# Silu slices of a background generator get a slot of their own, and the order of a selective scan's side work is rearranged

## The chip, the cores and the metric

The kernel runs on one core of a Trainium2 chip. The metric is device time in microseconds (us) of one execution, the median of several runs. Five engines of the core matter here: TensorE (PE in the profile), VectorE (DVE), ScalarE (ACT), GpSimd (POOL) and SyncE (SP), whose queue issues the DMAs. Each engine works through its own instructions in the order in which the program lists them, and waits on semaphores for the others.

## The reference

Sixteen images of 64 x 64 x 96 go through two residual blocks, all in float32.

```python
x = x + _L0_conv_ref(_gn(x), L0_conv_W1, L0_conv_b1, L0_conv_W2, L0_conv_b2, L0_conv_coef)
x = x + _L1_conv_ref(_gn(x), L1_conv_in_proj_w, L1_conv_conv_w, L1_conv_conv_b, ...)
```

The first block upsamples twofold by Fourier transform, applies a two-layer perceptron with a quadratic activation, filters and downsamples. The second block is a state-space layer: an input projection, a 3 x 3 depthwise convolution with Silu, four scan directions over the 4,096 positions, a layer norm, a Silu gate and an output projection. Its core is

```python
delta = jax.nn.softplus(dts + dt_bias[None, :, :, None])
...
def step(h, inps):
    dt, ut, bt, ct = inps
    h = jnp.exp(dt[..., None] * As[None]) * h + (dt * ut)[..., None] * bt[:, :, None, :]
    y = jnp.einsum('bkdn,bkn->bkd', h, ct)
    return (h, y)
```

for 192 channels, 16 states and 4 directions.

## The kernel before, in words

**The scan loop.** `scan` (from line 615) cuts the work into units. A unit holds 32 channels x 4 states as 128 partitions, in two halves `e` of the channels, over `T` = 1,024 positions. Four units (`j`) make a block of all 16 states, six blocks a step, eight steps an image: 192 units an image, 3,072 in all. Directions are taken in pairs: the backward pair scans the same tiles from the end.

Per unit the engines do this:

- ScalarE, `decay` (L755): `da` = exp(delta x A), 128 x 1024, into one of two buffers in PSUM (pool `sc_aps`, `bufs=2`).
- GpSimd, `drive` (L761): `b` = dtu x B for both halves at once, 128 x 2048, two units ahead; `b` has four buffers.
- VectorE, `recur` (L770 forward, L772 backward): the recurrence, by a scan instruction. Half 1 writes its result over `b`, half 0 over `da`.
- The product of the state with C: half 0 on VectorE (L924), half 1 on GpSimd (L915). Every fifth unit (`SHARE = 5`, `odd_here`), half 1 scans into `da` as well and its product is done on VectorE too (L906), so that GpSimd has one product less.
- ScalarE or VectorE, `keep` (L778): a copy of the last column, the state for the next step.
- TensorE, `read_out` (L794): sums over states, a unit later, 16 small matmuls into `y`; after a block, ScalarE copies `y` out (`store`, L805).

In the program, a unit `n` runs: scan of half 1, `decay(n+1, 1)`, position 0; product of half 1 on GpSimd, `drive(n+2)`, scan of half 0, `read_out(n-1)`, position 1; product of half 0, `keep`, `decay(n+1, 0)`, perhaps the copy of `y`, position 2.

**The side work.** Everything else is written as Python generators, whose pieces are put between the scan's instructions at the three positions of each unit, by `Background.slot`. A generator counts the weight of its pieces (1, or `HEAVY` = 2) and is given its next piece whenever it is behind an even spread: `SLICES` = 550 weights over the 576 positions of an image for `front` and `finish`, `PSLICES` = 71 over the 72 positions of a step for `project`. A piece that yields `WAIT` is followed by one that may stand at position 2 only.

- `front(mi)` does the first block of the next image and the start of the second. It works in strips of `PP` = 25 upsampled rows: `fetch_x` loads pieces `xr` of the image (L303), TensorE widens them (L324), groups of `PG` = 5 rows go through the perceptron (L365, L348, L377), then the rest. Its last part is the convolution with nine taps (L482), then a matmul for the gate (L494), then one slice with `Silu` for both (L500, L501). Silu is in another table of ScalarE than exp and log, so a table load stands on each side of it: one at L500, one by `preload_act_table_set(BOTH)` at L502. There are 12 such slices per image: 8 for the channels 0 to 127 (`i` = 0), 4 for the other 64 (`i` = 1, two halves of the image beside each other). The results go to DRAM, and `turn` (L467) makes a transposed copy `col`.
- `project(mi, pair, lc, out)` makes `delta` and `dtu` = delta x u for the next step: a projection `pp` (L655), copied to `pr` (L659), then for three channel groups a matmul (L666), a softplus in six ScalarE instructions (L674 to L681), a sum of four terms by identity matmuls on TensorE (L686), `dtu` on VectorE (L691), `delta` copied by ScalarE (L692), both stored to DRAM and later loaded spread over partitions (`spread`, L703).
- `finish(mi)` does the layer norm, gate and output projection of the image before.

The first `project` runs to its end before the scan begins, and so does the first `front`; the last `finish` runs after it. Loads and stores are all issued from SyncE's queue, in program order. Tiles named `piece` (11 buffers) are shared by all the side work; `b16` and `b18` have one buffer each and hold the image-sized tiles.

Of the kernel before, what the change touches and what calls it, by code (L numbers as in the profile page):

```python
# [54 lines left out]
UPS = 100  # L55
# [16 lines left out]
SLICES = 550  # L72
WAIT = -1
HEAVY = 2
# [5 lines left out]
def tile_two_blocks(  # L80
# [159 lines left out]
    def front(mi):  # L240
# [71 lines left out]
        o_last = None  # L312
        for p0 in range(0, UPS, PP):

            t1 = b18.tile([HW, PP, C], F32, name="t1", tag="b18")
            xr = fetch_x(0)
            for _ in range(3):
                yield
            for cg in range(3):
                u_ps = [bank([HW, 16, PP], "u_ps") for _ in range(2)]  # L320
                for k in range(16):
                    for a in range(2):
                        on = slice(64 * a, 64 * a + 64)
                        nc.tensor.matmul(  # L324
                            u_ps[a][:, k, :], lhsT=xr[k // 8][on, k % 8, :], rhs=up_s[on, p0:p0 + PP],
                            start=True, stop=True,
                        )
                    if k == 7:
                        yield
                if cg < 2:  # L330
                    xr = fetch_x(cg + 1)
                yield
                for a in range(2):
                    c0 = 48 * a + 16 * cg
                    nc.scalar.copy(t1[:, :, c0:c0 + 16], u_ps[a].rearrange("w c p -> w p c"))
                    yield
# [4 lines left out]
            for g in range(PP // PG):  # L341
# [8 lines left out]
                for j in range(HB + 1):  # L350
                    if j == 0 and o_last is not None:
                        keep_o(o_last)
                    elif j == 1 and len(t2) == 2:
                        square(0)
                        d_ps = narrow()
                        yield
                        sd = piece([128, PG * C], "sd")
                        nc.scalar.copy(sd, d_ps)
                    elif j:
                        square(j - 1)  # L360
                    if j == 2 and sd is not None:
                        stow(sd, row - 2 * PG)
                    if j < HB:
                        h_ps[j] = bank([128, PG * UPS], "h_ps")
                        nc.tensor.matmul(  # L365
                            h_ps[j], lhsT=w1t_s[:, 128 * j:128 * (j + 1)],
                            rhs=xu.rearrange("c p q -> c (p q)"), start=True, stop=True,
                        )
                    elif g < PP // PG - 1:
                        xu_ps = widen(t1, g + 1)  # L370
                    yield
# [89 lines left out]
        for i, n, tiles, both in ((0, 128, 8, 0), (1, 64, 4, 4)):  # L461
# [14 lines left out]
            for t in range(tiles):  # L476
                c_ps = bank([128, 8, HW], "c_ps")
                for tap in range(9):
# [8 lines left out]
                    if tap == 2 and turned is not None:  # L487
                        turn(*turned)
                    if tap % 3 == 2 and tap < 8:
                        yield HEAVY  # L490
# [13 lines left out]
                yield HEAVY  # L504
# [14 lines left out]
    def finish(mi):  # L519
# [19 lines left out]
        for t in range(8):  # L539
# [7 lines left out]
            for ob, n in ((0, 128), (1, 64)):  # L547
                oc = slice(128 * ob, 128 * ob + n)
                y_ps = bank([n, 8, HW], "yc")
                for i, (w, of) in enumerate(((pmat_s[:, 0, oc], y0), (pd_s[:, 0, oc], u0), (pd_s[:, 1, oc], yu))):  # L550
                    nc.tensor.matmul(  # L551
                        y_ps, lhsT=w, rhs=of.rearrange("c (h w) -> c h w", w=HW), start=(i == 0), stop=False
                    )
                if tail is not None:
                    tail = next(tail, None) and tail
# [3 lines left out]
                yield HEAVY  # L559
# [18 lines left out]
            yield HEAVY  # L578
# [5 lines left out]
            yield HEAVY  # L584
# [30 lines left out]
    def scan():  # L615


        with ExitStack() as es:
# [9 lines left out]
            banks.append(es.enter_context(tc.tile_pool(name="b_ps", bufs=2, space=PSUM)))  # L628
            aps = es.enter_context(tc.tile_pool(name="sc_aps", bufs=2, space=PSUM))
            yps = es.enter_context(tc.tile_pool(name="sc_yps", bufs=1, space=PSUM))  # L630
            gps = es.enter_context(tc.tile_pool(name="sc_gps", bufs=1, space=PSUM))

            def project(mi, pair, lc, out):
# [3 lines left out]
                out["rows"] = rows = dctx.tile([2, 2 * NS, T], F32, name="rows")  # L637
                out["delta"] = [dctx.tile([128, T], F32, name=f"delta_d{v}") for v in range(3)]
                out["dtu"] = [dctx.tile([128, T], F32, name=f"dtu_d{v}") for v in range(3)]
                xs_d = image[mi]["xs"]  # L640
                order = (0, 2, 1)

                def fetch_u(v, t):
                    uv = up_.tile([128, TB], F32, name="u")
                    nc.sync.dma_start(out=uv, in_=xs_d[v, :, lc * T + t:lc * T + t + TB])
                    return uv

                ahead_u = [fetch_u(v, 0) for v in order]
                for _ in range(4):
                    yield  # L650
                for t in range(0, T, TB):
                    u, ahead_u = dict(zip(order, ahead_u)), []
                    pp = gps.tile([128, TB], F32, name="pp", tag="g")
                    for v in range(3):
                        nc.tensor.matmul(pp, lhsT=xpt_s[:, pair, v, :], rhs=u[v], start=(v == 0), stop=(v == 2))  # L655
                    for _ in range(2):
                        yield
                    pr = pj.tile([128, TB], F32, name="pr")
# [3 lines left out]
                    for i, v in enumerate(order):  # L662
                        if i == 0:
                            yield
                        s = gps.tile([128, TB], F32, name="s", tag="g")
# [6 lines left out]
                        yield  # L672
                        e, d, m, w = (pj.tile([128, TB], F32, name=k) for k in ("e", "d", "m", "w"))
                        nc.scalar.activation(e, s, AF.Abs)  # L674
                        nc.scalar.activation(e, e, AF.Exp, scale=-1.0)
                        yield
                        nc.scalar.activation(m, s, AF.Relu)
                        nc.scalar.activation(w, e, AF.Identity, bias=one_s)
                        yield
# [3 lines left out]
                        s = gps.tile([128, TB], F32, name="s", tag="g")  # L683
# [3 lines left out]
                        for _ in range(3):  # L687
                            yield
                        dtu = pj.tile([128, TB], F32, name="dtu")
                        delta = pj.tile([128, TB], F32, name="delta")  # L690
# [6 lines left out]
                        if t + TB < T and i < 2:  # L697
# [40 lines left out]
            for _ in project(*steps[0], ctxs[0]):  # L738
                pass
            bc = {(what, 0, j): fetch_bc(ctxs[0], 0, j, what) for j in range(NQ) for what in range(2)}  # L740
            dtus = {0: fetch_dtu(ctxs[0], 0)}
            deltas = {(0, e): fetch_delta(ctxs[0], 0, e) for e in (1, 0)}
# [79 lines left out]
            class Background:  # L822

                def __init__(self, gen, slices, positions):
                    self.gen, self.slices, self.positions, self.at, self.n = gen, slices, positions, 0, 0
                    self.wait = False

                def slot(self, position):  # L830
                    self.at += 1
                    if self.wait and position < 2:
                        return
                    if self.gen is not None and self.n * self.positions < self.at * self.slices:
                        self.step()

                def step(self):
                    weight = next(self.gen, 0)
                    if weight == 0:
                        self.gen = None  # L840
                    else:
                        self.wait = weight == WAIT
                        self.n += 1 if weight in (None, WAIT) else weight

# [5 lines left out]
            ahead_gen = behind_gen = step_gen = nothing  # L850

            def slot(position):
                step_gen.slot(position)
                (ahead_gen if ahead_gen.gen is not None else behind_gen).slot(position)

            last = len(units) - 1
            def next_step(st, mi):

                nonlocal step_gen
                if st < len(steps):  # L860
                    if steps[st][0] > mi:
                        ahead_gen.drain()
                    step_gen = Background(project(*steps[st], ctxs[st]), PSLICES, 3 * per_step)
# [6 lines left out]
            storing = None  # L870

            for n, (st, bi, j) in enumerate(units):
# [29 lines left out]
                odd_here = n % SHARE == SHARE - 1  # L902
# [157 lines left out]
```

## Time and profile before

| | |
|---|---|
| time, median of 3 runs (lowest, highest) | 21502.07 us (21501.11, 21510.08) |
| profiled execution | 21508.85 us, span 21507.1 us |
| scan, first to last scan instruction | 536.2 to 21342.0 us |
| `da` decay, ScalarE L755 | 6144 of 1116 ns |
| scans, VectorE L770 and L772 | 6144 of 2280 to 2347 ns |
| products, VectorE L924 / L906 | 3072 of 1223 ns / 614 of about 1224 ns |
| `drive`, GpSimd L761 | 3072 of 4536 ns |
| product of half 1, GpSimd L915 | 2458 of 2361 ns |
| table loads in the scan, ScalarE L500 and L502 | 180 + 180 of 1283 ns |
| DMA | 4277 MB, mean 199 GB/s |

In the profile's lines, `DVE b L770 <- ACT da L755` reads: VectorE's instruction at line 770 that writes `b` waited for ScalarE's at line 755 that writes `da`. A group of instructions has its count after an `x`. Scans that write `b` are those of half 1, scans that write `da` those of half 0 (and of half 1 in every fifth unit). A window gives for each engine its busy us and, in brackets, its instructions. A timeline row has start, duration and engine; durations of two neighbours on VectorE and on ScalarE overlap by about 0.1 us.

### The profile page before, as it was taken

The numbers are of one execution on the slowest core, as the hardware profiler recorded it, in microseconds if no ns is written. First come the engines' busy times: TensorE is split into PE (matmuls) and PEld (weight loads), VectorE is DVE, ScalarE is ACT, GpSimd is POOL, SyncE is SP. The second block draws the span as 40 slices with busy tenths as digits, with TensorE's granted clock in tenths as the row PEclk, the third lists the DMA queues.
The fourth block names the chain that finished last, engine by engine and source line by source line (L and its number), as shares of the span: only waits on it lengthen the run. The fifth ranks groups of instructions, "written<-read, shape, count | busy, mean of one in ns | idle before, by whom it ended". The sixth has DMA issues, their size and how long they took to land. (4 is left out here: it accounts for less than half of the span.)

```text
span 21507.1 us, 273615 instructions
## 1 busy us (share of the span) xinstructions
PE 16918.9 (79%) x98988; PEld 7271.3 (34%) x98988; DVE 19512.2 (91%) x12983; ACT 13741.5 (64%) x20546; POOL 19511.8 (91%) x5538
## 2 busy tenths in 40 slices
PE   7776877878878788787878778788787888878855
PEld 4423324233332333324333242333423333243221
DVE  0999999999999999999999999999999999999997
ACT  3666666667666666666666666676666666666553
POOL 0999999999999999999999999999999999999996
PEclk8887888888889888898888888888898888888877
DMA  2565565656656566565655656566565665656654
GB/s 74 180 207 184 199 224 187 217 192 204 217 189 227 187 218 203 187 228 183 219 197 200 224 191 215 192 208 215 185 227 187 211 203 192 230 184 217 222 186 140
DMA packets 1855466, 4277.13 MB, mean 199 GB/s; under 512 B 449438, under 2 KB 548670, under 8 KB 1852062
## 3 DMA queue, kind: packets, MB, share of 16 engines
q1 hardware_dynamic: 1854110, 4259.62, 58.8%
q8 instruction: 781, 12.80, 0.2%
q14 instruction: 575, 4.71, 0.1%
HBM read 3380.58 MB, written 878.18 MB: 198 GB/s over the span
## 5 line engine op out<-in xcount | busy, mean ns | idle before, releaser
L761 POOL TENSOR_TENSOR b<-dtu,bt 128x2048 f32<-128x2048 f32 x3072 | 13905.1, 4536 | 594.2 <-DMA dtu<-dtu_d 530.5
L755 ACT ACTIVATE da<-delta,a_s 128x1024 f32<-128x1024 f32 x6144 | 6852.3, 1116 | 2859.4 <-DVE b L924 888.2
L915 POOL TENSOR_TENSOR b<-b,ct 128x1024 f32<-128x1024 f32 x2458 | 5804.1, 2361 | 1235.6 <-DVE new L778 832.6
L794 PE MATMUL y<-b,fold_s 128*32 128x256 f32 x49152 | 3837.1, 435 | 1111.6 <-DVE b L924 551.4
L924 DVE TENSOR_TENSOR b<-da,ct 128x1024 f32<-128x1024 f32 x3072 | 3756.5, 1223 | 93.9
L770 DVE TENSOR_TENSOR_SCAN da<-da,new,b 128x1024 f32<-128x1024 f32 x1383 | 3246.5, 2347 | 282.8 <-ACT da L755 274.7
L772 DVE TENSOR_TENSOR_SCAN da<-da,new,b 128x1024 f32<-128x1024 f32 x1382 | 3242.4, 2346 | 125.5 <-ACT da L755 119.1
L794 PEld LDWEIGHTS y<-b,fold_s 128*32 128x32 f32 x49152 | 1392.0, 119 | 3857.0 <-issue 1333.0
L778 ACT COPY new<-da 128x1 f32<-128x1 f32 x2764 | 434.6, 157 | 2786.4 <-DVE b L924 2294.7
L772 DVE TENSOR_TENSOR_SCAN b<-da,new,b 128x1024 f32<-128x1024 f32 x922 | 2157.9, 2341 | 47.0 <-ACT da L755 46.1
L770 DVE TENSOR_TENSOR_SCAN b<-da,new,b 128x1024 f32<-128x1024 f32 x921 | 2156.6, 2342 | 41.1 <-ACT da L755 39.5
L482 PE MATMUL c_ps<-xgp,wtap_s 96*128 96x512 f32 (+1 forms) x4608 | 1721.3, 642 | 203.6 <-ACT row L500 199.1
L686 PE MATMUL s<-w,ident_s 128*128 128x512 f32 x1536 | 1175.4, 857 | 872.0 <-ACT w L681 752.3
L666 PE MATMUL s<-pr,dtw_s 128*128 128x512 f32 x1536 | 939.0, 696 | 544.6 <-ACT delta L692 328.0
L365 PE MATMUL h_ps<-xu,w1t_s 96*128 96x500 f32 x1920 | 1059.4, 652 | 306.7 <-ACT hsq L348 124.2
L377 PE MATMUL o_ps<-w2c_s,hsq 128*100 128x96 f32 x9600 | 1031.9, 266 | 170.0 <-ACT hsq L348 143.7
L772 DVE TENSOR_TENSOR_SCAN da<-da,b 128x1024 f32<-128x1024 f32 x461 | 1055.9, 2291 | 118.4 <-ACT da L755 116.7
L770 DVE TENSOR_TENSOR_SCAN da<-da,b 128x1024 f32<-128x1024 f32 x460 | 1053.4, 2290 | 106.5 <-ACT da L755 104.3
L377 PEld LDWEIGHTS o_ps<-w2c_s,hsq 128*100 128x100 f32 x9600 | 966.1, 178 | 357.2 <-ACT hsq L348 184.9
L686 PE MATMUL s<-e,ident_s 128*128 128x512 f32 x1536 | 1022.9, 755 | 0.0
L482 PEld LDWEIGHTS c_ps<-xgp,wtap_s 96*128 96x128 f32 (+1 forms) x4608 | 600.1, 172 | 1154.9 <-issue 873.0
L787 PE MATMUL y<-y,ident_s 128*128 128x512 f32 x768 | 534.1, 784 | 538.6 <-ACT yt L805 537.1
(128 smaller groups left out, 21920.7 us busy)
## 6 DMA issues: line engine op xcount, KB each, us to landing
dtu<-dtu_d SPq DMA_DIRECT2D x1536, 512.0 KB
delta<-delta_d SPq DMA_DIRECT2D x1536, 512.0 KB
bt<-rows SPq DMA_DIRECT2D x1024, 512.0 KB
ct<-rows SPq DMA_DIRECT2D x1024, 512.0 KB
u<-xs_d SPq DMA_DIRECT2D x896, 256.0 KB
dtu_d<-dtu SPq DMA_DIRECT2D x768, 256.0 KB
delta_d<-delta SPq DMA_DIRECT2D x768, 256.0 KB
xr<-in_x SPq DMA_DIRECT2D x768, 128.0 KB
```

The source lines that it names most:

```text
L365: nc.tensor.matmul(h_ps[j], lhsT=w1t_s[:, 128 * j:128 * (j + 1)], rhs=xu.rearrange("c p q -> c (p q)"), start=True, stop=True,)
L377: nc.tensor.matmul(o_ps[:, p, :], lhsT=hsq[j][:, UPS * p:UPS * (p + 1)], rhs=w2c_s[:, j, :], start=(j == 0), stop=(j == HB - 1),)
L482: nc.tensor.matmul(c_ps[p:p + n], lhsT=wtap_s[:, tap, 128 * i:128 * i + n], rhs=xgp[:, h0:h0 + 8, dx:dx + HW], start=(tap == 0), stop=(tap ...
L666: nc.tensor.matmul(s, lhsT=dtw_s[:, pair, v, :], rhs=pr, start=True, stop=True)
L686: nc.tensor.matmul(s, lhsT=ident_s, rhs=of, start=(k == 0), stop=(k == 3))
L755: nc.scalar.activation(da, deltas[n // NQ, e], AF.Exp, scale=a_s[:, k, g, units[n][2]:units[n][2] + 1])
L761: nc.gpsimd.tensor_mul(b, dtus[n // NQ], bt.unsqueeze(1).to_broadcast([128, 2, T]))
L770: nc.vector.tensor_tensor_scan(out, da, b, before, ALU.mult, ALU.add)
L772: nc.vector.tensor_tensor_scan(out[:, ::-1], da[:, ::-1], b[:, ::-1], before, ALU.mult, ALU.add)
L794: nc.tensor.matmul(y[32 * q:32 * q + 32, e, :], lhsT=fold_s, rhs=b[:, e, QT * q:QT * q + QT], start=(pair == 0 and j == 0 and e == 0), sto ...
L915: nc.gpsimd.tensor_mul(h, h, bc[1, r, j])
L924: nc.vector.tensor_mul(bs[n][:, 0, :], h, bc[1, r, j])
```

## The change

- `Background` no longer skips positions itself. One function `slot` decides for both generators. A Silu slice (after `WAIT`) may come only at position 2, with no copy of `y` pending in the unit; then `full` keeps `project`'s pieces that follow a `BUSY` mark out of this position and the next, and `full_unit` makes the next unit one with both products on VectorE. A `project` that is behind may have two pieces at one position, if neither follows a `BUSY`.
- Units with both products come by `credit`: one is taken at every fifth unit as before, and one forced by a slice is paid back later.
- In `project`, the pieces with ScalarE work are marked `BUSY`.
- The convolution is cut into pieces of two taps (weight 1) instead of three (weight 2), the 64-channel part comes first, and several `HEAVY` yields of `finish` become plain ones, one of them new. `SLICES` is 499.
- `fetch_x` is called earlier: two fetches are in flight, and those of the next strip start in the last group of the strip before.
- The first `project` becomes two generators, one for each half of the 1,024 positions, that take turns; the second works in tiles of its own (`far_u`, `far_w`), in the two image-sized buffers. PSUM for it comes from a pool of its own with four banks. The first loads for the scan are issued once both halves have made their first channel group.

```diff
-SLICES = 550
+SLICES = 499
 WAIT = -1
+BUSY = -2
...
+        asked = []
         for p0 in range(0, UPS, PP):
...
-            xr = fetch_x(0)
-            for _ in range(3):
-                yield
+            if not asked:
+                asked += [fetch_x(0), fetch_x(1)]
+                for _ in range(3):
+                    yield
             for cg in range(3):
+                xr = asked.pop(0)
...
-                if cg < 2:
-                    xr = fetch_x(cg + 1)
+                if cg == 0:
+                    asked.append(fetch_x(2))
...
+                    if j >= 2 and g == PP // PG - 1 and p0 + PP < UPS:
+                        asked.append(fetch_x(j - 2))
...
-        for i, n, tiles, both in ((0, 128, 8, 0), (1, 64, 4, 4)):
+        for i, n, tiles, both in ((1, 64, 4, 4), (0, 128, 8, 0)):
...
-                    if tap == 2 and turned is not None:
+                    if tap == 3 and turned is not None:
                         turn(*turned)
-                    if tap % 3 == 2 and tap < 8:
-                        yield HEAVY
+                    if tap % 2 == 1:
+                        yield
...
-                        yield
+                        yield BUSY
                         e, d, m, w = (make(k) for k in ("e", "d", "m", "w"))
                         nc.scalar.activation(e, s, AF.Abs)
                         nc.scalar.activation(e, e, AF.Exp, scale=-1.0)
-                        yield
+                        yield BUSY
...
-            for _ in project(*steps[0], ctxs[0]):
-                pass
...
+            far_u = b16.tile([128, 4, TB], F32, name="far_u", tag="b16")
+            far_w = b18.tile([128, 6, TB], F32, name="far_w", tag="b18")
...
+            with tc.tile_pool(name="side_ps", bufs=4, space=PSUM) as side:
+                todo = [project(*steps[0], ctxs[0], side, 0), project(*steps[0], ctxs[0], side, TB, far.get)]
+                while todo:
+                    todo = [g for g in todo if next(g, todo) is not todo]
+                    if ctxs[0]["made"] >= 2 and not dtus:
+                        bc[0, 0, 0] = fetch_bc(ctxs[0], 0, 0, 0)
+                        dtus[0] = fetch_dtu(ctxs[0], 0)
+                        for e in (1, 0):
+                            deltas[0, e] = fetch_delta(ctxs[0], 0, e)
...
             def slot(position):
-                step_gen.slot(position)
-                (ahead_gen if ahead_gen.gen is not None else behind_gen).slot(position)
+                nonlocal full, full_unit
+                back = ahead_gen if ahead_gen.gen is not None else behind_gen
+                back.at += 1
+                step_gen.at += 1
+                gate = back.said == WAIT and back.due() and position == 2 and storing is None
+                if gate:
+                    full, full_unit = 2, n + 1
+                if step_gen.due() and not (full and step_gen.said == BUSY):
+                    light = step_gen.said != BUSY
+                    step_gen.step()
+
+                    if light and step_gen.due() and step_gen.said != BUSY:
+                        step_gen.step()
+                if back.due() and (gate or back.said != WAIT):
+                    back.step()
+                full = max(full - 1, 0)
...
-                odd_here = n % SHARE == SHARE - 1
+
+                credit += 1
+                odd_here = n == full_unit or credit >= SHARE
+                if odd_here:
+                    credit -= SHARE
```

## The prediction, made before the change was run

> **What bounds the kernel now.** I read the page's busy times first, then what VectorE and GpSimd wait for inside the scan (536 to 21342 us), then one image cut into four stages, then timelines.
>
> ```profile
> PE 16918.9 (79%) x98988; PEld 7271.3 (34%) x98988; DVE 19512.2 (91%) x12983; ACT 13741.5 (64%) x20546; POOL 19511.8 (91%) x5538
> ```
>
> The first five lines of VectorE's waits in the scan and the first of GpSimd's (us in total, times, longest):
>
> ```profile
> DVE da L770 <- ACT da L755: 379.0, 366, 3.4
> DVE da L772 <- ACT da L755: 235.8, 240, 4.0
> DVE dtu L691 <- PE s L686: 235.0, 129, 13.3
> DVE b L772 <- ACT da L755: 177.6, 88, 4.7
> DVE b L770 <- ACT da L755: 72.6, 58, 22.0
> ```
>
> ```profile
> POOL b L915 <- DVE new L778: 832.6, 438, 16.0
> ```
>
> VectorE and GpSimd are equally busy, and each idles about 1,300 us of the scan's 20,806. But VectorE hardly waits for GpSimd (23 us in all), while GpSimd waits for VectorE. So VectorE's chain sets the time: its work plus its waits for ScalarE (865 us) and TensorE (235 us). Time saved on GpSimd alone is worth nothing until those waits are gone.
>
> The stages of the image scanned from 4450 us on: its units 0 to 95, 96 to 139 (the Silu slices of the next image), 140 to 167, 168 to 191.
>
> ```profile
> core 0: us, PE busy (x) PEld busy (x) DVE busy (x) ACT busy (x) POOL busy (x), PEclk, DMA share, GB/s
> 4449.80:5101.50 651.70, 502.79 (x3706) 261.05 (x3706) 605.81 (x399) 434.42 (x699) 611.25 (x174) 0.82 0.58 195
> 5101.50:5407.90 306.40, 256.63 (x1192) 95.11 (x1192) 275.30 (x189) 218.61 (x300) 279.01 (x80) 0.89 0.63 206
> 5407.90:5595.30 187.40, 168.70 (x717) 55.42 (x718) 183.06 (x135) 113.16 (x171) 178.05 (x51) 0.93 0.70 233
> 5595.30:5748.80 153.50, 125.41 (x572) 41.04 (x570) 152.30 (x93) 90.25 (x115) 150.22 (x44) 0.89 0.66 216
> ```
>
> VectorE idles 46, 31, 4 and 1 us in them: there is little to gain after unit 140.
>
> A Silu slice that happens to stand before a unit with both products on VectorE, on ScalarE and then on VectorE:
>
> ```profile
> 2714.99 1.12 ACT L755 ACTIVATE da<-delta,a_s 128x1024 f32<-128x1024 f32 x1
> 2716.13 1.28 ACT L500 ACT_TABLE_LOAD   x1
> ...
> 2718.62 1.28 ACT L502 ACT_TABLE_LOAD   x1
> ...
> 2720.10 1.12 ACT L755 ACTIVATE da<-delta,a_s 128x1024 f32<-128x1024 f32 x1
> ```
>
> ```profile
> 2717.14 1.23 DVE L906 TENSOR_TENSOR b<-da,ct 128x1024 f32<-128x1024 f32 x1
> 2718.28 2.35 DVE L772 TENSOR_TENSOR_SCAN da<-da,new,b 128x1024 f32<-128x1024 f32 x1
> 2720.66 1.22 DVE L924 TENSOR_TENSOR b<-da,ct 128x1024 f32<-128x1024 f32 x1
> ```
>
> The next decay ends at 2721.22, the product at 2721.88: VectorE does not wait, with 0.6 us to spare.
>
> **What the Trainium skill says.** "ScalarE: Activation LUTs", What ACT_TABLE_LOAD costs, has about 1,283 ns for a load and some 1,380 ns of drain with it. The trace agrees on the load (1.28 us), but shows no drain beside it: the block of two loads and two activations takes 3.8 us here (2716.13 to 2719.90). "Perfetto Trace Analysis", Tensor Engine Instruction, says ScalarE, VectorE and GpSimd are strict FIFO; the decays behind the Silu block bear it out. "SBUF — State Buffer", two separate sides, says a VectorE instruction with two SBUF inputs and a GpSimd instruction lock each other out. The 96x1 product at line 236 fits: median 4.1 us, longest 12.0. Its count doesn't change; only its alignment to GpSimd will.
>
> **The Silu slices.** There are 180 in the scan. I joined each with VectorE's idle time before the first scan two units later, the first instruction that needs a decay queued behind it: 239 us in all. With nothing else in the slice and TensorE in time, 60 lose 0.08 us each; 15 followed by a unit with both products lose nothing. The loss is in three other groups: softplus pieces in the same slot (81 us), a y copy there (25 us), and 48 that wait for the convolution's last matmuls (ScalarE's row waits 107.8 us for them), which lose 127 us. In the changed program's order every one of the 180 has only the two loads and the two activations between its decays, and the following unit has both products. The first two groups go: -106 us. The TensorE group shrinks. Its last piece before the slice is 2 matmuls, not 4, of 0.97 us (in units 98 to 115 of the image above, 64 full-width matmuls, two records each, occupied TensorE for 61.8 us); so a row that came 3.0 us late comes about 1.1 late, and 0.6 is spare: 0.5 us at perhaps 60 slices, 30 us. Bounds 0 and 130 (no better than now). Together -209.
>
> **Second scans.** Of the 615 us before scans that write `da`, 479 us are 477 units that lose 1.00 us each: there the decay of half 0 was given the PSUM bank of half 1, so it starts only when this unit's first scan ends. Counting banks in the changed program gives 527: +50 us. In units 0 to 95 this is 1.3 us less per image (288 against 309 of them in the run); in 96 to 139 it is 12 per image against 7.2. The change doesn't touch the cause.
>
> **dtu.** 235 us wait for the softplus sums on TensorE, 73 of them in units 108 to 114, where three-tap pieces stand ahead. With two-tap pieces I take 2 us per image for 4.8 in that stage and 1.3 less per image elsewhere; the TensorE work per unit is only slightly more even (392 two-unit stretches above 12 us against 453, by durations of the trace). Bounds: all 235 stays, or 100 is left. The softplus steps themselves move little: 75 are held back, 153 pairs share a slot, nearly all of them DMA issues or a bare allocation.
>
> **The units with both products.** 614 in both kernels: they move. In 96 to 139 they become 13 for 9; the debt leaves 141 to 167 with none. An ordinary unit is 5.89 us of VectorE (starts 2.36, 2.37, 1.14 apart, and a copy in three of four) and 6.80 of GpSimd (4.49 and 2.31); one with both is 6.91 and 4.49.
>
> - Units 96 to 139, VectorE: before 35 x 5.89 + 9 x 6.91 + 44 x 0.15 (dtu) = 275.0, idle 32.5 by the mean over images, 307.5; measured mean 307.8. After: 31 x 5.89 + 13 x 6.91 + 6.6 = 279.0; idle 12 second scans, 2 Silu, 2 dtu, 1.3 others, 3.3 in gaps under 0.1 us: 20.6; in all 299.6. GpSimd needs 269. So -8.2 per image: 12 us of waits less, 4 us of work more.
> - Units 140 to 167: GpSimd becomes the bound, 27 x 6.80 + 4.49 = 188.1 against 189.0 measured (mean). VectorE needs some 183 and runs ahead.
> - Units 168 to 191: the last stage of an image now holds more of `finish` (it ends at unit 190, not 185). VectorE 159 less the 5 it is ahead, against 153.3. Both stages: -0.5.
> - Units 0 to 95: -1.3 and -1.3 as above.
>
> Sum: -11.3 per image, 15 images: -170 us.
>
> **First projection.** Now 430 to 536 us: six softplus rounds of 12 us in series, 515, then DMAs; the first decay waits until 533.97 for its delta. After: the second half's u goes into the buffer of `col`, whose 2 MB must first be stored (10 us at the page's mean of 199 GB/s); that holds both, since the halves alternate on TensorE. Then three double rounds of 19 us (7.8 ScalarE, 11 TensorE) and 8 us for `pp`: 430 + 10 + 8 + 57 = 505, with delta and dtu fetched long before. First scan at 508: -25, bounds -10 and -45. Earlier xr fetches in the first front: TensorE waits 7.1 us for them: -5. Inside the scan they are covered.
>
> Smaller weights and `SLICES` 499 only spread the same work: `front` ends at unit 141 for 135, `finish` still ends inside its image. The tail is the same.
>
> **Sum.** -170 - 30 = -200. From the profiled execution's 21508.9 us: 21309; the median of the runs shown is 6.8 lower: 21302.
>
> **Rivals.**
> 1. TensorE is late for the slices all the same. Pieces now come one a slot, and 105 of 180 slices stand one slot after the last piece (75 before). For: 48 waits now. Against: half-size pieces. If 105 lose 0.9 us and GpSimd's stretch costs 5 us more an image (95 + 75): 21302 + 170 - 30 = 21442, hardly a gain.
> 2. Slower: fetches of xr in the last group of a strip ask for pieces while all 11 are in use, and SyncE's queue, in order, holds delta loads behind them. Now decays wait 60.3 us for delta; SyncE already waits up to 13.0 us for a piece's reader. It decides when each of 3 strips holds delta loads 6 us past their lead: 18 x 15 = 270, so 21572. Against: the count of xr loads that wait for TensorE hardly rises (208 for 197).
> 3. More gain: slices lose nothing, dtu waits drop to 100, the projection gives 45: 21302 - 30 - 75 - 20 = 21177.
> 4. The delays do nothing because softplus isn't due near the slices: excluded, the changed program's order shows the slices bare.
>
> **Chances.** Forecast 0.58 (own range 21220 to 21400), rival 1 0.16, rival 2 0.09, rival 3 0.17. A measurement tells 0.2% (43 us) from no change. Rival 1 splits about evenly across 21459, so faster 0.83, same 0.08, slower 0.09. The range leaves out most of rival 2 and the ends of 1 and 3: 21120 to 21470.
>
> **What would show it.** First-scan waits (`b` L770, L772) fall from 250 to near 50; waits of `da` scans rise a little, from 615 towards 665; GpSimd without a gap in units 141 to 167; the first scan near 508 us. It is wrong if row still waits for c_ps over 100 us with the first scans idle, or if decays wait for delta much above 60 us.

## The result and the profile after

| | before | after |
|---|---|---|
| median (lowest, highest), us | 21503.11 (21501.11, 21510.08) | 21328.53 (21321.19, 21346.15) |
| profiled execution, its span | 21508.85, 21507.1 | 21326.15, 21324.4 |
| start of the scan; its length | 536.2; 20805.8 | 495.9; 20662.7 |

The ratio is 0.992, interval 0.9906 to 0.9934: faster by 175 us, against 200 forecast. Of the 183 us between the two profiled executions, 40 come from the earlier start of the scan and 143 from a shorter scan. The new numbers of the lines spoken of: decay L788, drive L794, scans L803 (forward) and L805 (backward), products L972, L954 and L963, dtu L702, row L506, the norm's product L237.

The page's busy times after, to compare with the first line shown before:

```profile
PE 16949.4 (79%) x98988; PEld 7262.1 (34%) x98988; DVE 19510.9 (91%) x12983; ACT 13759.8 (65%) x20546; POOL 19511.8 (91%) x5538
```

VectorE has as much to do as before, to 1.3 us. The gain is in its waits. Each unit has two scans: the first is that of half 1, the second that of half 0. VectorE's waits after, in the scan (us in total, times, longest):

```profile
DVE da L803 <- ACT da L788: 305.7, 318, 1.9
DVE da L805 <- ACT da L788: 287.4, 251, 4.5
DVE dtu L702 <- PE s L697: 143.6, 95, 13.8
...
DVE b L805 <- ACT da L788: 98.2, 69, 3.8
...
DVE b L803 <- ACT da L788: 20.8, 22, 1.7
```

First scans (`b`) lose 119 us for 250, `dtu` 144 for 235, while the `da` scans still lose 593 us for 615. The four stages of the image scanned from 4400 us on, cut at the same units as before:

```profile
4399.60:5033.10 633.50, 496.10 (x3702) 258.62 (x3702) 602.97 (x393) 424.06 (x660) 607.57 (x173) 0.84 0.57 195
5033.10:5344.30 311.20, 250.52 (x1183) 91.86 (x1184) 286.90 (x195) 226.15 (x338) 272.49 (x77) 0.87 0.59 194
5344.30:5531.90 187.60, 157.13 (x693) 51.63 (x692) 177.35 (x131) 114.29 (x168) 185.14 (x55) 0.92 0.78 259
5531.90:5689.30 157.40, 139.70 (x610) 45.40 (x608) 154.24 (x95) 93.43 (x120) 153.22 (x44) 0.95 0.66 219
```

The stage that was to gain, the second, became longer: 311 us for 306, with VectorE busy 287 for 275. The first became 18 us shorter. Means over 14 images, the second to the fifteenth, say the same (us per image; the last three columns are kernels of the experiments below):

| units | before | after | before, own buffers | after, own buffers | best kernel |
|---|---|---|---|---|---|
| 0 to 95 | 655.3 | 637.7 | 633.9 | 624.9 | 624.8 |
| 96 to 139 | 307.6 | 310.7 | 296.6 | 309.6 | 297.4 |
| 140 to 167 | 189.2 | 188.6 | 185.4 | 189.2 | 185.8 |
| 168 to 191 | 153.3 | 157.5 | 153.3 | 157.0 | 153.0 |

A Silu slice that TensorE did not reach in time, on ScalarE, VectorE and TensorE (`row` is what the slice's first activation writes, `c_ps` the convolution's result that it reads):

```profile
5256.94 1.28 ACT L506 ACT_TABLE_LOAD   x1
5262.42 0.69 ACT L506 ACTIVATE row<-c_ps,convb_s 128x512 f32<-128x512 f32 x1 [4.19 <-PE c_ps L488]
```

```profile
5266.60 2.35 DVE L805 TENSOR_TENSOR_SCAN b<-da,new,b 128x1024 f32<-128x1024 f32 x1 [3.45 <-ACT da L788]
```

```profile
5250.52 4.65 PE L488 MATMUL c_ps<-xgp,wtap_s 96*128 96x512 f32 x8
5255.01 1.02 PE L697 MATMUL s<-w,ident_s 128*128 128x512 f32 x2
...
5257.59 1.02 PE L697 MATMUL s<-m,ident_s 128*128 128x512 f32 x2
5258.44 1.88 PE L488 MATMUL c_ps<-xgp,wtap_s 96*128 96x512 f32 x4
5261.26 1.13 PE L488 MATMUL c_ps<-xgp,wtap_s 96*128 96x512 f32 x2
```

The reader sees an empty ScalarE: after the table load it stands 4.19 us for the last taps, and the decay behind it makes VectorE's next scan 3.45 us late, in spite of the 1.23 us product put in between. On TensorE the four sums of a softplus (5255.0 to 5258.4) lie between two pieces of the convolution: keeping softplus from ScalarE's slot does not keep it from TensorE's queue. There are 60 such late rows in the scan, 124 us in all; before there were 48, with 108 us.

### The profile page after: what moved, and what is told of

Read it like the earlier page. It is cut to its first block, busy times and chain, and to the rows that moved or that the text cites. A ratio compares the mean times of both kernels' runs of the same rounds, so it can differ in the third digit from the quotient of the medians.

```text
span 21324.4 us, 273404 instructions
## 1 busy us (share of the span) xinstructions
PE 16949.4 (79%) x98988; PEld 7262.1 (34%) x98988; DVE 19510.9 (91%) x12983; ACT 13759.8 (65%) x20546; POOL 19511.8 (91%) x5538
## 5 line engine op out<-in xcount | busy, mean ns | idle before, releaser
L794 POOL TENSOR_TENSOR b<-dtu,bt 128x2048 f32<-128x2048 f32 x3072 | 13908.5, 4537 | 593.7 <-DMA dtu<-dtu_d 468.4
L788 ACT ACTIVATE da<-delta,a_s 128x1024 f32<-128x1024 f32 x6144 | 6846.5, 1116 | 3074.8 <-DVE b L972 947.3
L963 POOL TENSOR_TENSOR b<-b,ct 128x1024 f32<-128x1024 f32 x2458 | 5809.4, 2363 | 1052.8 <-DVE new L811 786.2
L972 DVE TENSOR_TENSOR b<-da,ct 128x1024 f32<-128x1024 f32 x3072 | 3756.5, 1223 | 91.8
L803 DVE TENSOR_TENSOR_SCAN da<-da,new,b 128x1024 f32<-128x1024 f32 x1383 | 3246.6, 2348 | 206.5 <-ACT da L788 198.8
L805 DVE TENSOR_TENSOR_SCAN da<-da,new,b 128x1024 f32<-128x1024 f32 x1361 | 3194.1, 2347 | 200.8 <-ACT da L788 188.6
L805 DVE TENSOR_TENSOR_SCAN b<-da,new,b 128x1024 f32<-128x1024 f32 x943 | 2208.1, 2342 | 112.8 <-ACT da L788 81.0
L803 DVE TENSOR_TENSOR_SCAN b<-da,new,b 128x1024 f32<-128x1024 f32 x921 | 2156.3, 2341 | 10.5 <-ACT da L788 9.9
L488 PE MATMUL c_ps<-xgp,wtap_s 96*64 96x512 f32 (+1 forms) x4608 | 1721.4, 632 | 180.4 <-ACT row L506 175.1
L805 DVE TENSOR_TENSOR_SCAN da<-da,b 128x1024 f32<-128x1024 f32 x482 | 1103.8, 2290 | 106.7 <-ACT da L788 98.9
L803 DVE TENSOR_TENSOR_SCAN da<-da,b 128x1024 f32<-128x1024 f32 x460 | 1053.5, 2290 | 107.1 <-ACT da L788 106.9
L488 PEld LDWEIGHTS c_ps<-xgp,wtap_s 96*64 96x64 f32 (+1 forms) x4608 | 582.9, 169 | 1115.4 <-issue 849.2
```

Source lines behind the costliest of these rows:

```text
L488: nc.tensor.matmul(c_ps[p:p + n], lhsT=wtap_s[:, tap, 128 * i:128 * i + n], rhs=xgp[:, h0:h0 + 8, dx:dx + HW], start=(tap == 0), stop=(tap ...
L788: nc.scalar.activation(da, deltas[n // NQ, e], AF.Exp, scale=a_s[:, k, g, units[n][2]:units[n][2] + 1])
L794: nc.gpsimd.tensor_mul(b, dtus[n // NQ], bt.unsqueeze(1).to_broadcast([128, 2, T]))
L803: nc.vector.tensor_tensor_scan(out, da, b, before, ALU.mult, ALU.add)
L805: nc.vector.tensor_tensor_scan(out[:, ::-1], da[:, ::-1], b[:, ::-1], before, ALU.mult, ALU.add)
L963: nc.gpsimd.tensor_mul(h, h, bc[1, r, j])
```

## The experiments

Times are medians; "loss" and "gain" in the text are against the changed kernel, 21328.5 us, unless another kernel is named. The kernel before, run again beside each group of experiments, took 21497 to 21504 us. Where waits are counted by kind, VectorE's idle time before each scan is summed over all units.

**The changed kernel with the old pace.**

```diff
-SLICES = 499
+SLICES = 550
```

> The changed kernel with SLICES 550 again, so that the side work is handed out at 0.95 weights a position as before, not 0.87. Theory (the gain of units 0 to 95, 17.6 us an image, comes from spreading the first block's work thinner): that stage returns from 637.7 us an image to about 648, and the time to 21430. Rival (it comes from the earlier image loads and the new order of pieces, whatever the pace): the stage stays within 3 us of 637.7, the time within 30 us of 21328. Second-scan waits don't tell them apart: 525 units share a bank here, 527 in the changed kernel.

21481.1 us (ratio to before 0.9992, 0.9983 to 1.0): with the old pace the whole gain is gone, although the first scan still begins at 494.7 us. Per image, units 0 to 95 take 10.8 us more (648.5, as the theory had it), 96 to 139 take 4.6 more and 168 to 191 take 4.6 less.

Most of the loss stands at one place. The front now ends at unit 128, and `finish` issues its six loads of `ycol` (3 MB) in units 129 to 131, mostly right ahead of the `delta` that the second scan of unit 132 needs. One image, on SyncE's queue (`SPq`), ScalarE and VectorE:

```profile
5314.13 2.04 SPq L200 DMA_DIRECT2D ycol<-y_d  x3
5316.27 0.55 SPq L715 DMA_DIRECT2D delta<-delta_d  x1
```

```profile
5328.37 2.15 ACT L788 ACTIVATE da<-delta,a_s 128x1024 f32<-128x1024 f32 x2 [11.37 <-DMA delta<-delta_d]
```

```profile
5329.52 2.36 DVE L805 TENSOR_TENSOR_SCAN da<-da,new,b 128x1024 f32<-128x1024 f32 x1 [9.62 <-ACT da L788]
```

From 5311.0 to 5328.4 us the DMA engines were busy 0.99 of the time. Over all images VectorE idles 159 us before this one scan. With 499 the six loads stand in units 142 to 144, where the second scan of unit 144 waits 52 us. The difference, 107 us, is about two thirds of what the old pace costs. This was read from the traces; no run moved these loads alone.

**A pace half way,** at which the front ends at unit 135, as in the kernel before.

```diff
-SLICES = 499
+SLICES = 523
```

> The changed kernel with SLICES 523: front then ends at unit 135 of an image, as in the kernel before (141 with 499, 128 with 550). Theory (the pace sets the waits roughly in proportion): halfway between 21328 and 21481, 21400, and units 0 to 95 near 643 us an image; so about 75 us of the change's 175 are its thinner pace and the rest its slices and first projection. Rival (only falling short of room at the end, or chance in which unit each piece lands, matters): 21330 or 21480, or outside both.

21473.8 us (0.9988, 0.9981 to 0.9995), so 145 us lost and not half of the 153. Here units 0 to 95 take 637.2 us, as with 499, but 96 to 139 take 10.3 us more and 140 to 167 3.2 more. The loss has another place than with 550: decays wait only 9 us for `delta`, but in units 96 to 139 `dtu` waits 9.0 us per image for 3.0, first scans wait 3.0 us more, and the second norm's product (line 237) takes 7.1 us for 4.4. So the time doesn't follow the pace in proportion: each pace puts pieces next to other instructions, and 499 is the best of three. Why the softplus sums come later with 523 wasn't found out.

**Without the forced unit:** the second product of half 1 on VectorE comes every fifth unit only.

```diff
-                odd_here = n == full_unit or credit >= SHARE
+                odd_here = credit >= SHARE
```

> The changed kernel without the forced unit: both products go to VectorE at every fifth unit only. Theory of the change (the forced unit hides the end of the Silu block): first-scan waits behind the slices rise from 97 us by 0.4 to 1.0 us at 180 slices, 70 to 180 us, less 66 us of VectorE work that no longer falls into units 96 to 139: 21330 to 21440. Rival (a slice that stands bare loses nothing even before an ordinary unit, as 60 of them did before the change with 0.08 us each): waits stay near 97 us, and the time falls by some 40 us, to 21290.

21427.8 us (0.9961, 0.9946 to 0.9976): 99 us lost, as the theory of the change had it. First scans behind a slice wait 199 us for 97, units 140 to 167 take 191.3 us for 188.6.

**Without the hold:** softplus pieces may share the slice's slot.

```diff
-                if step_gen.due() and not (full and step_gen.said == BUSY):
+                if step_gen.due():
```

> The changed kernel without the hold: softplus pieces may stand in a slice's position and the next. Theory (softplus beside a slice costs what it did before the change, 81 us at 18 slices with softplus in the same position): 75 pieces come back, first-scan waits rise by 60 to 100 us, 30 units fewer share a bank: 21360 to 21400. Rival (only pieces ahead of the Silu block on ScalarE matter, and the forced unit covers the rest): within 25 us of 21328.

21401.0 us (0.995, 0.9935 to 0.9965): 72 us lost. First scans behind a slice wait 187 us, although only 34 rows are late for TensorE (91 us). So what the change names does what it says: forced unit and hold take 102 and 90 us of waits behind a slice.

**Three-tap pieces again,** with the weight of a slice's tile as it is in the change.

```diff
-                    if tap == 3 and turned is not None:
+                    if tap == 2 and turned is not None:
                         turn(*turned)
-                    if tap % 2 == 1:
-                        yield
+                    if tap % 3 == 2 and tap < 8:
+                        yield HEAVY
```

> The changed kernel with the convolution in pieces of three taps, weight 2, as before the change; the weight of a tile is the same 6, so the pace is the same. Theory (two-tap pieces keep TensorE nearer its time): the row's wait for c_ps rises from 124 to over 180 us, the dtu waits from 145 towards 200, and the time by 50 to 110 us, to 21380 to 21440. Rival (the last piece stands one position before the slice either way, and TensorE's order in between decides): row's wait between 90 and 150 us, time within 30 us of 21328.

21306.2 us (21283 to 21311, below every run of the changed kernel): smaller pieces bring nothing. The waits of `row`, first in the changed kernel, then with the larger pieces:

```profile
ACT row L506 <- PE c_ps L488: 124.0, 60, 4.2
```

```profile
ACT row L506 <- PE c_ps L488: 51.8, 15, 3.5
```

Both theories had put it at 90 us or more. How long before its slice the last piece stands decides whether a row can be late at all. In the traces a row is late only where that piece comes behind the `read_out` of the slice's own unit in TensorE's order, which is one position ahead of the slice. In the changed kernel 105 of the 180 slices stand so, and 60 of them are late; in the kernel before it is 48 of 75, here 15 of 30. No other slice is late in any of the three. That fits the weights: a piece with weight 2 is followed by two free slots, one with weight 1 by one.

**A PSUM buffer of its own for each half.** The pool `sc_aps` has two buffers, and a decay is given one by the order in which the program frees them, not by its half. In 477 units of the kernel before, and 527 after, the decay of half 0 has the buffer that this unit's first scan still reads. On ScalarE and VectorE of the changed kernel it looks like this:

```profile
5055.23 1.12 ACT L788 ACTIVATE da<-delta,a_s 128x1024 f32<-128x1024 f32 x1 [0.33 <-DVE b L805]
```

```profile
5052.92 2.28 DVE L805 TENSOR_TENSOR_SCAN b<-da,b 128x1024 f32<-128x1024 f32 x1
5055.23 0.15 DVE L811 COPY new<-b 128x1 f32<-128x1 f32 x1
5056.38 2.30 DVE L805 TENSOR_TENSOR_SCAN da<-da,b 128x1024 f32<-128x1024 f32 x1 [1.00 <-ACT da L788]
```

The first scan ends, only then the decay (1.12 us) runs, and the second scan begins 1.00 us late. Here ScalarE stood idle for 0.33 us before that decay; in 368 of the 527 units it stands 0.9 us or more until the first scan ends, and nothing but the buffer is in the way. The edit, in the changed kernel and then in the kernel before:

```diff
-            aps = es.enter_context(tc.tile_pool(name="sc_aps", bufs=2, space=PSUM))
+            aps = es.enter_context(tc.tile_pool(name="sc_aps", bufs=1, space=PSUM))
...
-                da = aps.tile([128, T], F32, name="da")
+                da = aps.tile([128, T], F32, name="da", tag=f"da{e}")
```

> The changed kernel with a PSUM buffer of its own for each half's decay, so that no decay of half 0 is given half 1's bank. Theory (the 527 shared-bank units cost 1.0 us each on VectorE's chain, 558 us before second scans): these waits fall below 100 us and the time to about 20940, with GpSimd's idle time falling from 1179 to under 800 us. Rival (the decay would be late anyway, since ScalarE has to finish the copy of the state before it): second-scan waits stay over 400 us and the time within 80 us of 21328.

> The kernel before, with a PSUM buffer of its own for each half's decay and nothing else changed. Theory (the shared bank is a cost of its own, of the same size in both kernels): the changed kernel gained 234 us for 527 units, 0.44 us a unit; 477 units give 212 us, so about 21290, and second-scan waits fall from 540 us to 60 to 230. Rival (it matters only once the slices stand bare): less than 80 us, 21420 or more.

With it the changed kernel takes 21094.1 us (0.9808, 0.9793 to 0.9822), the kernel before 20965.4 (0.9753, 0.9738 to 0.9767): 234 and 538 us gained. Waits before second scans fall from 589 to 229 us and from 540 to 186, so the shared buffer was the cause of most of them.

The sizes expected were wrong: 20940 was put for the changed kernel, and then 21290 for the kernel before, on the view that a unit with a shared buffer costs both the same. In the kernel before, first scans wait 80 us less too and `dtu` 56 less. In the changed kernel first scans wait 56 us more, and the norm's products (line 237) keep VectorE busy for 194 us instead of 115.

And the order turns round: on equal buffers the change makes the kernel 129 us slower, although its first scan comes 55 us earlier. The windows of units 96 to 139 of one image, first the kernel before with own buffers, then the changed one with them:

```profile
5004.80:5301.40 296.60, 249.68 (x1192) 93.17 (x1192) 274.79 (x189) 218.96 (x300) 279.06 (x80) 0.92 0.65 213
```

```profile
4969.70:5279.10 309.40, 250.54 (x1185) 92.03 (x1186) 286.86 (x195) 226.73 (x338) 272.58 (x77) 0.88 0.59 195
```

VectorE idles about 22 us in both. The changed kernel has 12 us more of VectorE work there: 4.4 units more with both products, worth 1.02 us each, and 8.1 us of the front's second norm (line 237), which the new pace moved here from units 0 to 95. Over the whole scan this product did not only move: the norms' products take 194 us for 130 in the kernel before with own buffers, and another small sum (line 260, `lin`) 38 for 12. These 89 us are half of the 178 us by which the scan is now longer; what holds such instructions up is shown in the last section.

**Own buffers, without the forced unit and with the old pace.** The edits are those of above, together.

> The changed kernel with a PSUM buffer of its own for each half's decay, and without the forced unit (its second product goes by the count of five alone). Compared with the changed kernel with own buffers (21094 us). Theory (the forced unit is a debt: 4.5 us of VectorE work per image and a GpSimd bill paid in units 140 to 167, which only paid while the waits at the shared bank were there to be shifted): faster by 40 to 120 us, near 21010 us, with the stage 96 to 139 back from 309.6 to about 303 us per image and the first scans' waits behind a Silu up from 96 to about 200 us. Rival (the forced unit hides the Silu and its two table loads whatever the buffers): slower by 60 to 100 us, near 21180 us, as it was with the shared bank (+99 us). Neither: within 30 us of 21094, the bill and the waits cancel.

> The changed kernel with own PSUM buffers for each half's decay and the old pace (550 in place of 499). With the shared bank the old pace cost 152 us. Theory (the pace acts on waits at the shared bank and on what is late for TensorE, the first of which is gone): within 40 us of 21094. Rival (the pace of 499 keeps TensorE in time for dtu and row whatever the buffers): slower by about 150 us, near 21240 us, with the second norm's products and the rows' waits back (late rows 75 and 169 us as with the shared bank).

Without the forced unit: 21083.4 us, 11 us under 21094.1, which is no difference. First scans behind a slice wait 81 us more (177 for 96), and units 96 to 139 take 1.1 us per image less and 140 to 167 1.3 more. Both theories fell: the work that the forced unit adds to VectorE and the waits that it saves cancel. With the old pace: 21168.1 us, 74 us slower, which lies between the two theories. The second scan of unit 132 again waits for its `delta`, 180 us in all, where 51 us are lost at unit 144 with the pace of 499. So that wait doesn't need the shared buffers; the rest of the scan is shorter with the old pace here.

**The norm's product on ScalarE,** in the changed kernel with own buffers.

```diff
-        nc.vector.tensor_mul(nb, nmean, rg)
+        nc.scalar.activation(nb, nmean, AF.Identity, scale=rg)
```

> The changed kernel with a buffer for each half's decay, and the 96x1 product nb moved from VectorE to ScalarE (an activation with a scale). With the buffers alone it takes 21094 us, and VectorE is busy 194 us in these 30 products of the scan. Theory (VectorE with two SBUF inputs is locked out while GpSimd works): the 194 us leave VectorE and the time falls by 100 to 170 us, to 20925 to 20995. Rival (the long busy time is a wait for rg that the profile charges to the instruction): ScalarE's result comes as late, and the time stays within 40 us of 21094.

20931.0 us (0.9737, 0.9722 to 0.9751): 163 us gained by moving 32 products of 96 numbers, 30 of them in the scan. VectorE was busy with them for 194 us in that kernel.

**The best of these together.** The kernel before with own buffers, the norm's product on ScalarE, and of the change only the first projection in two halves (the edits are those shown).

> The kernel before with three parts: own PSUM buffers for each half's decay, the norms' product (96x1, two operands in SBUF) on ScalarE, and of the change only the first projection in two halves. Theory (the parts add: 20965 us with own buffers alone, about 50 us off the first scan's start, 110 to 160 us of VectorE time at the product): 20760 to 20820 us, first scan near 495 us. Rival (GpSimd, with 766 us of gaps left in the kernel before with own buffers, becomes the bound as VectorE's work goes): 20850 to 20920 us, with GpSimd idle under 600 us in the scan.

20857.4 us (0.9704, 0.9689 to 0.9718), 108 us under the kernel before with own buffers. Neither theory holds as put: the time is in the rival's range, but GpSimd still idles 710 us in the scan, so that it is the bound isn't shown. The product's 130 us became only 78 in the scan. The groups of VectorE show where 23 of them went: another tiny instruction with two operands in SBUF, the sum of 96x96 at line 259 (`lin`), grew from 13 to 36 us.

**That sum with one operand in PSUM.**

```diff
-        nc.scalar.activation(lin, mt_s, AF.Identity, scale=rg)
+        lin_ps = bank([C, C], "lin_ps")
+        nc.scalar.activation(lin_ps, mt_s, AF.Identity, scale=rg)
...
-        nc.vector.tensor_add(lin, lin, ident_s[0:C, 0:C])
+        nc.vector.tensor_add(lin, lin_ps, ident_s[0:C, 0:C])
```

> As the kernel of own buffers, norms' product on ScalarE and first projection in two halves (20857 us), but the sum of 96x96 at the start of each front (lin plus the identity; two operands in SBUF, median 2.8 us, 36 us in all) reads its first operand from PSUM, where ScalarE now writes it. Theory (only an instruction with two SBUF operands is held up while GpSimd works): the sum takes 0.24 to 0.3 us, VectorE has 31 us less to do, 20815 to 20835 us. Rival (any VectorE instruction that happens to come after a GpSimd one is held, and the stretch falls to the next one): the sum still has a median over 1 us, or another product of VectorE grows by as much, and the time stays within 10 us of 20857.

20812.7 us (0.9676, 0.9663 to 0.969), 45 us less and 2 us below the theory's range. One line of the group in each kernel, without and with the edit (ns, shortest/median/longest):

```profile
L259 DVE TENSOR_TENSOR lin<-lin,ident_s x16: 243/2792/3386, 40.9 to 18251.1; 96x96 f32<-96x96 f32 x16
```

```profile
L260 DVE TENSOR_TENSOR lin<-lin_ps,ident_s x16: 243/244/254, 40.1 to 18210.1; 96x96 f32<-96x96 f32 x16
```

The theory held: none of the 16 is held up once an operand lies in PSUM, and no other group of VectorE's instructions in the scan grew by more than 1.4 us. This kernel is the fastest, 516 us under the changed one.

## Why the prediction was right, and where it wasn't

The total was right to 27 us, its parts less so. Per image the four stages gave -17.6, +3.1, -0.6 and +4.2 us, -10.9 together, where -2.6, -8.2 and -0.5 had been put, -11.3 together. That these sums agree is luck.

- **Silu slices, -209 predicted.** Measured -142: first scans behind a slice wait 97 us for 239. The groups that shared a slot went: the 120 slices that TensorE reached in time lose 0.6 us together, and the runs without hold and without forced unit show that both are needed for it. The failed term is the TensorE group: "a row that came 3.0 us late comes about 1.1 late", 30 us left. 60 rows came late, by 2.1 us in the mean, and cost 97 us; before, 48 had come late by 2.2. The term counted the size of the last piece only, neither its distance from the slice nor the sums queued between. So rival 1 was half true: its 105 slices one slot behind their last piece are where the rows are late, and its "against", the half-size pieces, was wrong, since larger pieces gave 15 late rows.
- **Second scans, +50 predicted.** Measured +49 (540 to 589 us); in units 96 to 139 12.6 us per image, where 12 were put. The close agreement is in part chance. The 527 units lose 558 us for 479, so 79 more, of which 37 come from the late `delta` at unit 144; a late one at unit 44, worth 38 us before, is gone. The view shown for it, the waits of all `da` scans, fell from 615 to 593 instead of rising, since it also holds the first scans of units with both products, which now stand behind the slices. It was the wrong row to name as evidence. That "the change doesn't touch the cause" was right, but the cause turned out to be worth more than the change.
- **dtu, -61 predicted.** Measured -91 (236 to 145), inside the bounds, in another place: -5.0 us per image in units 0 to 95, where -1.3 was put.
- **Units 96 to 139, -8.2 per image predicted.** Measured +3.1. First scans give 8.8 us, the forced units cost 4.5 and second scans 4.2 more, as worked out within a few us. What was left out is 4.4 us of the second norm's product, which the pace moved in. The sentence that the smaller weights and the pace "only spread the same work" is the step that failed: the old pace costs 153 us, most of it at one late load.
- **Units 0 to 95, -2.6 predicted.** Measured -17.6: 6.3 less at the norm's product (4.4 of it moved on), 5.0 less for dtu, 3.9 less before second and 3.0 before first scans. With the old pace 10.8 of these are lost again.
- **Units 140 to 191, -0.5 predicted.** 140 to 167 took 188.6 us, where GpSimd's work made 188.1; GpSimd idles 3.3 us there for 10.7. 168 to 191 lost 4.2: work of `finish` came later, which the step named and priced lower. Its own figures, -0.9 and +0.7, make -0.2 and not -0.5.
- **First projection, -25 predicted, and -5 for earlier fetches in the first front.** Measured -40.3 together, and none of it in the first front: ScalarE's work on that ends at 426.6 us, and at 424.5 before. ScalarE's instructions at the start of the projection and at three later points of the second half:

```profile
442.87 0.69 ACT L670 ACTIVATE far_u<-pp,bumps_s 128x512 f32<-128x512 f32 x1 [1.88 <-DMA rows<-pr]
...
459.14 0.59 ACT L703 COPY far_w<-s 128x512 f32<-128x512 f32 x1 [2.79 <-DVE far_w L702]
...
475.81 0.59 ACT L703 COPY far_w<-s 128x512 f32<-128x512 f32 x1 [2.85 <-DVE far_w L702]
...
492.67 0.59 ACT L703 COPY far_w<-s 128x512 f32<-128x512 f32 x1 [2.85 <-DVE far_w L702]
```

  The second half's `pp` is there at 442.9, not 448, and only 2.6 us after that of the first half; a double round takes 16.7 us, not 19. So the 10 us put for the store of `col` and the rounds were both sized too long.
- **Rival 2** (SyncE's queue): decays wait longer for `delta` than the 60.3 us in 19 cases of before:

```profile
ACT da L788 <- DMA delta<-delta_d: 114.0, 48, 5.6
```

  The line that was to betray it, "much above 60 us", was crossed without the time getting worse. But 95 us of it fall on units 144 and 148, beside the loads of `finish`, which is not what the rival named. Only 16.5 us, at unit 64, lie beside the fetches of `xr`, and VectorE loses 5 us there, where 270 had been put.

The line named for a wrong prediction, `row` waiting over 100 us with the first scans idle, was met too, and the first scans were indeed idle, 97 us. Two of the four signs named for a right one failed: first scans (`b`) wait 119 us, not near 50, and the `da` scans 593, not towards 665. The total came out because units 0 to 95 and the first projection gave what the slices and the later stages did not. Of rival 3 the projection alone came true, with 40 of its 45 us.

## What to carry to other kernels

Before arranging work around a wait, look for the small wait that repeats: 527 waits of about 1 us at one buffer were worth more than the whole arrangement (234 us for 175), and once they were gone its sign turned. Give each role a buffer of its own where a pool's order of release decides who waits for whom. After a move, sum each stage's busy time as well as its waits, and look at single units: a pace "only" moves work, but the work that it moves may cost more beside its new neighbours, and one load in a bad place cost 159 us.

## What was not expected of the hardware

A VectorE instruction on 96 numbers with both operands in SBUF takes 0.16 us ahead of the scan, where GpSimd stands idle, and up to 12.0 in it, and it is counted as busy time, not as waiting (ns, shortest/median/longest, in the kernel before):

```profile
L236 DVE TENSOR_TENSOR nb<-nmean,rg x32: 155/4122/12027, 38.5 to 19441.6; 96x1 f32<-96x1 f32 x32
```

The Trainium skill, "SBUF — State Buffer", SBUF: two separate sides, says that a VectorE instruction with two SBUF inputs and a GpSimd instruction that reads SBUF exclude each other, and that the one that starts first keeps the other out for its whole length. The traces agree: in the kernel before, each of the 30 products in the scan ends 11 to 21 ns after an instruction of GpSimd has ended. But one GpSimd instruction needn't be all: within the longest product, four of GpSimd's ended, the last two of which are

```profile
3784.43 8.96 POOL L761 TENSOR_TENSOR b<-dtu,bt 128x2048 f32<-128x2048 f32 x2
```

```profile
3781.38 12.03 DVE L236 TENSOR_TENSOR nb<-nmean,rg 96x1 f32<-96x1 f32 x1
```

The runs give the size of it: moving 32 such products to ScalarE gained 163 us, and the sum with a single operand in PSUM took 243 to 254 ns (above). When one such instruction left VectorE, the next in line grew: `lin` took 38 us in the changed kernel with own buffers, and 72 once the norm's product had gone.
